# A softmax over heads: summing part of the heads by accumulating transfers

## The chip, the cores and the metric

The kernel runs on one core of a Trainium2 chip. Four of its engines compute: TensorE (PE, with its weight loads as PEld) multiplies matrices into PSUM, VectorE (DVE), ScalarE (ACT) and GpSimd (POOL) work on elements. SyncE (SP) issues transfers, and so can ACT and POOL. Each engine works through its own queue in order and waits on semaphores for the others. The metric is device time in microseconds; the median of three runs counts.

## The reference

The program is four layers, each a cross-attention and a feed-forward network, over 1024 tokens of 128 features and a context of 6404 tokens. The change touches the attention of layer 2 only. What is special in it is that the softmax runs over the 16 heads (axis 1), and not over the keys:

```
qh, kh, vh = split_heads(q @ Wq.T), split_heads(k @ Wk.T), split_heads(v @ Wv.T)   # 16 heads of 8
scores = einsum('bhqd,bhkd->bhqk', qh, kh) / sqrt(8)
attn   = softmax(scores, axis=1)                  # over the heads
heads  = einsum('bhqk,bhkd->bhqd', attn, vh)
x      = x + merge_heads(heads) @ Wo.T
```

So for each key and each query there are 16 exponentials, and all 16 must be summed before any of them can be divided by the sum.

## The kernel before

The function is attn_heads. The work is cut into steps: 1024 queries are two halves of 512 (HALF), the 6404 keys are 51 blocks of 128 (the last has 4), so there are N = 102 steps. A step holds 16 tiles of 128 keys by 512 queries, one for each head. It goes through K = 8 slots, and a slot k handles a pair of heads, 2k and 2k+1. The exponentials of four heads share one tile, so a step has four tiles e0 to e3 of 128 x 2048 float32, each with two buffers.

The loop over slots is a software pipeline written out by hand: under manual_schedule the engines TensorE, ScalarE, VectorE and GpSimd execute in the order in which the program calls them, and nothing is moved by a planner. In one turn of the loop, for slot number `slot` (step i, pair k), these are called:

- least_made: 11 slots ahead, TensorE makes rough scores in bfloat16 in a PSUM tile (pair_ps, one buffer of two banks), and ScalarE casts them to the tile lb (three buffers; L1461). least_so_far: VectorE keeps the smallest over the heads (low, L1469; mneg at the end of a step, L1474). This shifts the exponent for safety.
- exps: TensorE makes the scores of the pair (x_ps, two buffers; L1548) and adds the shift through an identity matmul (L1552). ScalarE takes the exponential into e (L1555).
- first_summed (L1564): TensorE adds one head to a PSUM bank (s_ps) by a matmul with the identity. It takes one head in each slot, eight in a step: heads 0 to 5, 10 and 11 of the 16.
- summed: VectorE adds the other four pairs: pairs 3 and 4 into acc (L1579), then pair 6 and pair 7 onto it (L1582), then folds the two halves of acc (L1585) and adds them to sum (L1586).
- out_of_bank (L1591): in slot 1 of the next step ScalarE copies the bank s_ps into sum.
- inverted (L1598, L1599): ScalarE takes the logarithm of the sum and exp of minus that; improved (L1604, L1605): one Newton step on VectorE. This is 1 / sum.
- shared (L1611): VectorE multiplies a tile e of four heads by it, in every second slot, from slot SHARED = K + 3 of the step on.
- values (L1618): in every second slot from VALUES = K + 6 on, TensorE multiplies such a tile by the values of its heads (vz, spread by ScalarE at L1535) into o_ps. make_values (L1521) makes the values of four steps at a time.

Keys are loaded from DRAM by SyncE two steps ahead (load_keys, L1508). In the second half of the loop the feed-forward network of the first half of the tokens is called between the slots (along); its norm has one small POOL instruction (rstd, L116). POOL does nothing else in the loop but two memsets of a key tile for the blocks of 4 keys (L1506). All 8 PSUM banks are taken: two by pair_ps, four by x_ps, one each by o_ps and s_ps.

Of the kernel before, what the change touches and what calls it, by code (L numbers as in the profile page):

```python
# [10 lines left out]
F32 = mybir.dt.float32  # L11
# [5 lines left out]
ALU = mybir.AluOpType  # L17
# [3 lines left out]
P = 128  # L21
S = 1024
NT = S // P
HALF = 512
# [3 lines left out]
NH = 16  # L28
# [18 lines left out]
class Net:  # L47
# [1317 lines left out]
    def attn_heads(self, ctxT, tiles, before, along):  # L1365
# [13 lines left out]
        nc, tc, a = self.nc, self.tc, self.a  # L1379
# [4 lines left out]
        K = NH // 2  # L1384
        scale = 8.0**-0.5
        with ExitStack() as st:
# [51 lines left out]
            steps = [(c, at, n, half) for half in range(2) for c, (at, n) in enumerate(keys)]  # L1438
            N = len(steps)
            lows, mnegs, es, accs, sums, firsts, invs, kts, outs = ({} for _ in range(9))  # L1440
# [5 lines left out]
            def least_made(slot):  # L1446

                i, k = divmod(slot, K)
                c, at, n, half = steps[i]
                m = self.pair_tile()  # L1450
                for t, (j, r) in enumerate(heads(k)):
                    nc.tensor.matmul(  # L1452
                        m[:n, t], kb[r, at : at + n], qn[r, j, ts(half, HALF)],
                        start=True, stop=True,
                    )
                if k == 0:
                    lows[i] = lp.tile([P, 2, HALF], BF16, tag="low", name="low")
                    t = lows[i]
                else:
                    t = lp.tile([P, 2, HALF], BF16, tag="lb", name="lb", bufs=3)  # L1460
                nc.scalar.copy(t[:n], m[:n])  # L1461
                return t
# [21 lines left out]
            pr = self.pool(st, "a2p", 2)  # L1484
# [3 lines left out]
            ps_s = self.pool(st, "a2ps_s", space=PSUM)  # L1488
# [13 lines left out]
            def load_keys(i):  # L1502
                _, at, n, _ = steps[i]
                kts[i] = pr.tile([P, 4, P], F32R, tag="kS", name="kS", bufs=3)
                if n < P:
                    nc.gpsimd.memset(kts[i].bitcast(F32), 0.0)  # L1506
                for g in range(4):
                    nc.sync.dma_start(  # L1508
                        out=kts[i][32 * g : 32 * g + 32, :, :n].bitcast(F32),
                        in_=kst[P * g : P * g + P, at : at + n].rearrange(  # L1510
                            "(j r) n -> r j n", j=4
                        ),
                    )
# [23 lines left out]
            def pair(i, k):  # L1537
                at = 2 * (k % 2)
                return es[i, k // 2][: steps[i][2], at : at + 2]

            def exps(slot):
                i, k = divmod(slot, K)
                c, at, n, half = steps[i]
                if k % 2 == 0:
                    es[i, k // 2] = e_tile(k // 2)
                s = ps_x.tile([P, 2, HALF], F32, tag="x", name="x_ps")
                for t, (j, r) in enumerate(heads(k)):
                    nc.tensor.matmul(  # L1548
                        s[:, t], kts[i][r, j], qS[r, j, ts(half, HALF)], start=True, stop=False
                    )  # L1550
                for t in range(2):
                    nc.tensor.matmul(  # L1552
                        s[:, t], self.identb, mnegs[i], start=False, stop=True
                    )
                nc.scalar.activation(pair(i, k), s[:n], AF.Exp)  # L1555

            def first_summed(slot):

                i, k = divmod(slot, K)
                if k == 0:  # L1560
                    firsts[i] = ps_s.tile([P, HALF], F32, tag="s", name="s_ps")
                n = steps[i][2]
                h = k if k < 6 else k + 4
                nc.tensor.matmul(  # L1564
                    firsts[i], self.ident[:n], es[i, h // 4][:n, h % 4],
                    start=k == 0, stop=k == K - 1,
                )

            def summed(slot):

                i, k = divmod(slot, K)
                if k == 0:
                    i -= 1
                if i < 0:
                    return
                n = steps[i][2]
                if k == 4:
                    accs[i] = pr.tile([P, 2, HALF], F32, tag="acc", name="acc")
                    nc.vector.tensor_tensor(accs[i][:n], pair(i, 3), pair(i, 4), ALU.add)  # L1579
                elif k in (6, 7):  # L1580
                    acc = accs[i][:n]
                    nc.vector.tensor_tensor(acc, acc, pair(i, k), ALU.add)  # L1582
                elif k == 0:
                    acc = accs[i][:n]
                    nc.vector.tensor_tensor(acc[:, 0], acc[:, 0], acc[:, 1], ALU.add)  # L1585
                    nc.vector.tensor_tensor(sums[i][:n], sums[i][:n], acc[:, 0], ALU.add)  # L1586

            def out_of_bank(i):
                n = steps[i][2]
                sums[i] = pr.tile([P, HALF], F32, tag="sum", name="sum", bufs=1)  # L1590
                nc.scalar.copy(sums[i][:n], firsts.pop(i)[:n])  # L1591

            def inverted(i):

                n = steps[i][2]
                invs[i] = pr.tile([P, HALF], F32, tag="inv", name="inv")
                r, t, s = invs[i][:n], accs[i][:n, 0], sums[i][:n]
                nc.scalar.activation(t, s, AF.Ln)  # L1598
                nc.scalar.activation(r, t, AF.Exp, scale=-1.0)  # L1599
# [13 lines left out]
            def values(i, j):  # L1613
                c, at, n, half = steps[i]
                if c == 0 and j == 0:
                    outs[half] = ps_o.tile([P, HALF], F32, tag="o", name="o_ps")
                for g in range(4):
                    nc.tensor.matmul(  # L1618
                        outs[half][32 * g : 32 * g + 32],
                        vz[i % 2][:n, ds(P * j + 32 * g, 32)], es[i, j][:n, g],  # L1620
                        start=c == 0 and j == 0, stop=c == NK - 1 and j == 3,
                    )
                if c == NK - 1 and j == 3:
                    ob = lp.tile([P, HALF], F32, tag="q32", name="ob")
                    nc.scalar.copy(ob, outs[half])
                    y = self.m_tile()
                    for t in range(4):
                        nc.tensor.matmul(
                            y[:, ts(t, P)], ob[:, ts(t, P)], wo, start=True, stop=True
                        )  # L1630
                    self.add_to_tokens(y, half)

            SHARED = K + 3
            VALUES = K + 6
            SLOTS = N * K
            kept = {}
            other = make_queries(1)
# [3 lines left out]
            for slot in range(SLOTS + 3 * K):  # L1641
                i, k = divmod(slot, K)
                if k == 0 and i + 2 < N:
                    load_keys(i + 2)
                if 1 <= i <= N and k == 1:
                    out_of_bank(i - 1)
                if slot + AHEAD < SLOTS:
                    kept[slot + AHEAD] = least_made(slot + AHEAD)
                if slot < SLOTS:
                    exps(slot)  # L1650
                if 0 < slot <= SLOTS:
                    first_summed(slot - 1)
                at = slot - VALUES
                if 0 <= at < SLOTS and at % 2 == 0:
                    values(at // K, at % K // 2)
                if 0 <= at + 2 < SLOTS and (at + 2) % K == 0:
                    spread_values((at + 2) // K)
                if 0 <= at + 5 < SLOTS and (at + 5) % (4 * K) == 0:
                    make_values((at + 5) // K)
                if slot - 1 + AHEAD in kept:  # L1660
                    least_so_far(slot - 1 + AHEAD, kept.pop(slot - 1 + AHEAD))
                if 0 < slot <= SLOTS + 1:
                    summed(slot - 1)
                if 1 <= i <= N and k == 2:
                    inverted(i - 1)
                if 1 <= i <= N and k == 3:
                    improved(i - 1)
                at = slot - SHARED
                if 0 <= at < SLOTS and at % 2 == 0:
                    shared(at // K, at % K // 2)  # L1670
                if 2 <= i < NK:
                    next(other, None)
                elif i >= NK + 4 and k % 2 == 0:
                    if next(along, None) == "other table":
                        exp_and_ln()
# [425 lines left out]
```

## Time and profile before

| What | Value |
|---|---|
| Time, median of three runs | 6065.93 us (6054.96 to 6070.65) |
| The profiled execution, its own time | 6077.67 us |
| Its span, first to last instruction | 6076.0 us |
| Busy in the span: PE, DVE, ACT, POOL | 91%, 79%, 69%, 16% |
| Mean granted clock of TensorE | 0.957 |
| First and last exponential of the loop (L1555) | 2413.9 and 4573.4 us |
| The loop's sums on TensorE, L1564 | 1632 rows, 850.4 us |
| Additions on VectorE, L1582 (4 of the 204 have 4 rows) | 204, 1216 ns each |
| Copies out of the bank, L1591 | 102, 593 ns each |
| POOL's own transfers (queue q0), whole program | 17.22 MB |

A float32 matmul shows as two rows in the profile, so 1632 rows are 816 sums, eight in each of 102 steps. A row that follows another on the same engine may start before the first has ended by the record, as the engines overlap the end of one instruction with the beginning of the next. For that reason the cost of an instruction in a full queue is read from start to start. In the answers "idle before" gives how long the engine stood before an instruction, and behind the arrow who released it. The granted clock is the share of full speed at which TensorE was allowed to run.

### The profile page before, as it was taken

To read this page: it belongs to the slowest core of one execution; us is meant where nothing else is said; L and a number is where in the kernel's file an instruction comes from. 1 tells how busy PE (TensorE), PEld (TensorE's weight loads), DVE (VectorE), ACT (ScalarE), POOL (GpSimd) and SP (SyncE) were. 2 spreads that over 40 slices of the span, in tenths; PEclk is the share of its full clock that TensorE was granted. 3 is DMA by queue.
4 is the path that set the end of the run, shared out by engine and by line. 5 is a ranking of instruction groups with operands and counts; after the bars stand their busy time and mean duration, and the time that the engine had idled before them with its cause. 6 is when DMAs were issued, how large, how long until landed. Compare 5 with 4: busy or idle time off the path is not lost. (4 is left out here: it accounts for less than half of the span.)

```text
span 6076.0 us, 77642 instructions
## 1 busy us (share of the span) xinstructions
PE 5513.2 (91%) x30144; PEld 2099.9 (35%) x30144; DVE 4771.1 (79%) x5417; ACT 4202.4 (69%) x5284; POOL 964.6 (16%) x687
## 2 busy tenths in 40 slices
PE   6999988899999998999999988899996899999987
PEld 2333335333333345333333322333332333333334
DVE  5555535888888844999999999999997888888834
ACT  3555544677777775888888877788874677777764
POOL 4888883100000010000000000000002000000001
PEclk9999998899999998999999999999996899999978
DMA  0000011100011041000000000000002100011001
GB/s 18 3 2 3 1 40 60 31 14 14 14 18 17 7 150 47 13 13 15 13 15 13 11 13 9 13 15 13 15 8 65 34 14 14 15 18 18 6 16 41
DMA packets 139333, 130.02 MB, mean 21 GB/s; under 512 B 30750, under 2 KB 120278, under 8 KB 137983
## 3 DMA queue, kind: packets, MB, share of 16 engines
q1 hardware_dynamic: 129894, 103.35, 7.8%
q0 software_dynamic: 5296, 17.22, 0.9%
q8 instruction: 239, 3.92, 0.3%
q10 hardware_dynamic: 3760, 4.36, 0.2%
q14 instruction: 144, 1.17, 0.1%
HBM read 102.18 MB, written 35.85 MB: 23 GB/s over the span
## 5 line engine op out<-in xcount | busy, mean ns | idle before, releaser
L994 DVE TENSOR_REDUCE mx<-pair_ps 128x2 f32<-128x1024 f32 x1612 | 1810.5, 1176 | 251.8 <-PE pair_ps L990 229.7
L1223 ACT ACTIVATE px<-x_ps 128x1024 f32<-128x1024 f32 x1088 | 1113.8, 1024 | 312.9 <-PE x_ps L1218 308.4
L1611 DVE TENSOR_TENSOR e<-e,inv 128x2048 f32<-128x2048 f32 (+1 forms) x408 | 932.0, 2285 | 10.8 <-DVE inv L1605 0.9
L1108 PE MATMUL o_ps<-px,v 128*32 128x512 f32 x4352 | 905.8, 621 | 0.0
L1108 PE MATMUL o_ps<-py,v 128*32 128x512 f32 x2176 | 898.3, 618 | 0.0
L990 PE MATMUL pair_ps<-kb,qz 64*128 64x512 bf16 (+1 forms) x3224 | 826.5, 386 | 53.7 <-DVE mx L994 36.9
L1223 ACT ACTIVATE py<-y_ps 128x512 f32<-128x512 f32 x1088 | 647.6, 595 | 327.2 <-PE y_ps L1218 323.6
L1555 ACT ACTIVATE e<-x_ps 128x1024 f32<-128x1024 f32 (+1 forms) x816 | 843.1, 1033 | 25.4 <-PE x_ps L1552 24.8
L1564 PE MATMUL s_ps<-e,ident 128*128 128x512 f32 (+1 forms) x1632 | 850.4, 603 | 0.3 <-ACT sum L1591 0.2
L1461 ACT CAST lb<-pair_ps 128x1024 bf16<-128x1024 f32 (+1 forms) x714 | 721.0, 1010 | 185.4 <-PE pair_ps L1452 136.1
L1218 PE MATMUL x_ps<-qS,kS 33*128 33x512 f32 x2176 | 713.1, 533 | 124.6 <-ACT px L1223 124.5
L400 POOL TENSOR_TENSOR acc<-acc,pt 128x1024 f32<-128x1024 f32 x256 | 601.9, 2351 | 65.3 <-ACT pt L389 51.0
L342 DVE TENSOR_REDUCE mx<-b_ps 128x2 f32<-128x1024 f32 (+1 forms) x306 | 341.1, 1115 | 344.7 <-PE b_ps L338 344.7
L1218 PE MATMUL y_ps<-qS,kS 33*128 33x512 f32 x1088 | 571.3, 525 | 5.7 <-ACT py L1223 5.7
L1469 DVE TENSOR_TENSOR low<-lb,low 128x1024 bf16<-128x1024 bf16 (+1 forms) x714 | 488.8, 685 | 33.1 <-ACT lb L1461 14.0
L1552 PE MATMUL x_ps<-mneg,identb 128*128 128x512 bf16 x1632 | 500.5, 389 | 0.1
L1452 PE MATMUL pair_ps<-qn,kb 32*128 32x512 bf16 (+1 forms) x1632 | 319.8, 387 | 168.2 <-ACT lb L1461 144.1
L1618 PE MATMUL o_ps<-e,vz 128*32 128x512 f32 (+1 forms) x3264 | 446.4, 620 | 9.8 <-DVE e L1611 9.8
L389 ACT ACTIVATE pt<-x_ps,bias 128x1024 f32<-128x1024 f32 x288 | 305.4, 1110 | 213.5 <-PE x_ps L384 198.5
L1218 PEld LDWEIGHTS x_ps<-qS,kS 33*128 33x128 f32 x2176 | 286.1, 192 | 461.9 <-ACT px L1223 215.9
L1548 PE MATMUL x_ps<-qS,kS 32*128 32x512 f32 x1632 | 418.2, 504 | 0.5 <-ACT e L1555 0.5
L990 PEld LDWEIGHTS <-qz 64*128 64x128 bf16 x3224 | 265.5, 94 | 341.5 <-issue 241.0
(387 smaller groups left out, 6115.5 us busy)
## 6 DMA issues: line engine op xcount, KB each, us to landing
kS<-kst SPq DMA_DIRECT2D x400, 64.0 KB
kS<-kd SPq DMA_DIRECT2D x120, 200.1 KB
w<-in_L_ffn_w SPq DMA_DIRECT2D x48, 256.0 KB
kst<-kd POOLq DMA_DIRECT2D x24, 512.0 KB, 13.7
kd<-kh SPq DMA_DIRECT2D x12, 512.0 KB
kd<-k SPq DMA_DIRECT2D x12, 512.0 KB
qS<-qd SPq DMA_DIRECT2D x256, 16.0 KB
kb<-in_L_ffn_w SPq DMA_DIRECT2D x16, 256.0 KB
```

The costliest lines, as they stand in the source:

```text
L400: nc.gpsimd.tensor_tensor(accs[u][:n], first[:n], pt[:n], ALU.add)
L990: nc.tensor.matmul(m[:, g, :n], qzs[u][r, ts(t, P)], kb[r, at : at + n], start=True, stop=True,)
L994: nc.vector.tensor_reduce(mxs[u][:, t, b], m[:, :, :n], AX.X, ALU.max)
L1108: nc.tensor.matmul(o[32 * j : 32 * j + 32], v[:, c, ds(VW * h, 32)], pt, start=i == 0, stop=c + 2 >= NK,)
L1218: nc.tensor.matmul(s[:, k], kS[p % 2][r, ts(c, P)], qS[u % 2][r], start=True, stop=True,)
L1223: nc.scalar.activation(pt[:, : len(some)], s[:, : len(some)], AF.Exp)
L1461: nc.scalar.copy(t[:n], m[:n])
L1469: nc.vector.tensor_tensor(low[:n], t[:n], low[:n], ALU.min)
L1552: nc.tensor.matmul(s[:, t], self.identb, mnegs[i], start=False, stop=True)
L1555: nc.scalar.activation(pair(i, k), s[:n], AF.Exp)
L1564: nc.tensor.matmul(firsts[i], self.ident[:n], es[i, h // 4][:n, h % 4], start=k == 0, stop=k == K - 1,)
L1611: nc.vector.tensor_tensor(e, e, r, ALU.mult)
```

## The change

The sum over the 16 heads of a step is divided in another way.

- VectorE adds pairs 0 and 1 into acc (first_added) in slot 2, and no other pair.
- Pairs 2, 3 and 4 are added to acc by three transfers that GpSimd's queue issues in slots 3, 4 and 5, from SBUF to SBUF with accumulation (more_added). Each is 128 rows of 4 KB, 512 KB. Each waits for the one before it, because all three add to the same tile.
- TensorE adds the last six heads, 10 to 15, in the bank: two in slot 6, one in slot 7, two in slot 0 of the next step and one in its slot 1 (late_summed).
- In slot 2 of the next step VectorE, right after the first_added of that step, folds acc and adds it to the bank, which it reads from PSUM directly. ScalarE's copy of the bank is gone.
- inverted, improved, shared and values come one slot later (SHARED = K + 4, VALUES = K + 7).

The diff, without the lines that are only removed text of the old functions:

```diff
+            late_heads = {6: (10, 11), 7: (12,), 8: (13, 14), 9: (15,)}
+            def late_summed(slot):
                 i, k = divmod(slot, K)
+                if k < 2:
+                    i, k = i - 1, k + K
+                if i < 0 or i >= N or k not in late_heads:
                     return
                 n = steps[i][2]
+                for h in late_heads[k]:
+                    if h == 10:
+                        firsts[i] = ps_s.tile([P, HALF], F32, tag="s", name="s_ps")
+                    nc.tensor.matmul(
+                        firsts[i], self.ident[:n], es[i, h // 4][:n, h % 4],
+                        start=h == 10, stop=h == NH - 1,
+                    )
+            def first_added(i):
                 n = steps[i][2]
+                accs[i] = pr.tile([P, 2, HALF], F32, tag="acc", name="acc")
+                nc.vector.tensor_tensor(accs[i][:n], pair(i, 0), pair(i, 1), ALU.add)
+            def more_added(i, k):
+                acc = accs[i][: steps[i][2]]
+                nc.gpsimd.dma_start(out=acc, in_=pair(i, k), accum_op=ALU.add)
+            def summed(i):
+                n = steps[i][2]
+                acc = accs[i][:n]
                 sums[i] = pr.tile([P, HALF], F32, tag="sum", name="sum", bufs=1)
-                nc.scalar.copy(sums[i][:n], firsts.pop(i)[:n])
+                nc.vector.tensor_tensor(acc[:, 0], acc[:, 0], acc[:, 1], ALU.add)
+                nc.vector.tensor_tensor(sums[i][:n], firsts.pop(i)[:n], acc[:, 0], ALU.add)
...
-            SHARED = K + 3
-            VALUES = K + 6
+            SHARED = K + 4
+            VALUES = K + 7
...
-                if 1 <= i <= N and k == 1:
-                    out_of_bank(i - 1)
...
-                if 0 < slot <= SLOTS:
-                    first_summed(slot - 1)
+                late_summed(slot)
...
-                if 0 < slot <= SLOTS + 1:
-                    summed(slot - 1)
+                if i < N and k == 2:
+                    first_added(i)
+                if i < N and k in (3, 4, 5):
+                    more_added(i, k - 1)
                 if 1 <= i <= N and k == 2:
+                    summed(i - 1)
+                if 1 <= i <= N and k == 3:
                     inverted(i - 1)
-                if 1 <= i <= N and k == 3:
+                if 1 <= i <= N and k == 4:
                     improved(i - 1)
```

More of the change, by code (lines that the diff above doesn't have):

```diff
@@ L1555, in exps @@
                 nc.scalar.activation(pair(i, k), s[:n], AF.Exp)
-            def first_summed(slot):
+            late_heads = {6: (10, 11), 7: (12,), 8: (13, 14), 9: (15,)}
+            def late_summed(slot):
                 i, k = divmod(slot, K)
[L1560 to L1574, printed above, removed]
+                if k < 2:
+                    i, k = i - 1, k + K
+                if i < 0 or i >= N or k not in late_heads:
                     return
                 n = steps[i][2]
[L1577 to L1586, printed above, removed]
@@ L1588, in out_of_bank @@
-            def out_of_bank(i):
-                n = steps[i][2]
+                for h in late_heads[k]:
[6 more added lines that the diff above has]
+            def first_added(i):
+                n = steps[i][2]
+                accs[i] = pr.tile([P, 2, HALF], F32, tag="acc", name="acc")
+                nc.vector.tensor_tensor(accs[i][:n], pair(i, 0), pair(i, 1), ALU.add)
```

## The prediction

> **What bounds the kernel now.** I read the page's slices first, then the loop by stretches, then VectorE, ScalarE and TensorE of two steps in order of time, then the transfers. The loop runs from 2413 to about 4591 us, slices 16 to 30 of 152 us each.
>
> ```profile
> DVE  5555535888888844999999999999997888888834
> ...
> PEclk9999998899999998999999999999996899999978
> ```
>
> By stretch (length, then busy us and instructions of PE, PEld, DVE, ACT, POOL, then clock, DMA share, GB/s):
>
> ```profile
> 2700.00:3300.00 600.00, 559.88 (x2895) 190.41 (x2893) 583.42 (x562) 506.51 (x600) 0.00 (x0) 1.00 0.06 14
> 3420.00:3900.00 480.00, 416.26 (x2034) 144.34 (x2035) 448.23 (x529) 356.67 (x422) 2.02 (x2) 0.95 0.05 12
> ```
>
> ```profile
> 3023.06 1.22 DVE L1579 TENSOR_TENSOR acc<-e,e 128x1024 f32<-128x1024 f32 x1
> ...
> 3027.00 1.22 DVE L1582 TENSOR_TENSOR acc<-acc,e 128x1024 f32<-128x1024 f32 x1
> 3028.13 2.28 DVE L1611 TENSOR_TENSOR e<-e,inv 128x2048 f32<-128x2048 f32 x1
> ...
> 3043.32 1.22 DVE L1579 TENSOR_TENSOR acc<-e,e 128x1024 f32<-128x1024 f32 x1
> ```
>
> One step is 3043.32 - 3023.06 = 20.26 us, and VectorE starts something new as soon as it can in all of it: 97% busy. The other two wait for it, and for each other:
>
> ```profile
> 3034.19 0.63 ACT L1598 ACTIVATE acc<-sum 128x512 f32<-128x512 f32 x1 [1.14 <-DVE sum L1586]
> 3034.85 0.63 ACT L1599 ACTIVATE inv<-acc 128x512 f32<-128x512 f32 x1
> 3035.39 0.99 ACT L1461 CAST lb<-pair_ps 128x1024 bf16<-128x1024 f32 x1
> 3036.28 1.03 ACT L1555 ACTIVATE e<-x_ps 128x1024 f32<-128x1024 f32 x1
> ```
>
> ```profile
> 3036.43 0.39 PE L1452 MATMUL pair_ps<-qn,kb 32*128 32x512 bf16 x2 [1.54 <-ACT lb L1461]
> 3036.44 0.50 PE L1548 MATMUL x_ps<-qS,kS 32*128 32x512 f32 x2
> 3036.87 0.61 PE L1552 MATMUL x_ps<-mneg,identb 128*128 128x512 bf16 x2
> 3037.32 1.02 PE L1564 MATMUL s_ps<-e,ident 128*128 128x512 f32 x2
> 3038.27 1.06 PE L1618 MATMUL o_ps<-e,vz 128*32 128x512 f32 x8
> 3039.26 0.39 PE L1452 MATMUL pair_ps<-qn,kb 32*128 32x512 bf16 x2
> ```
>
> There is one pair_ps tile, so TensorE begins no slot before ScalarE's cast of the slot before has ended. The starts give its prices: scores 0.88 (36.43 to 37.32), a head's sum 0.96, values 0.99. Each of 8 slots has one sum: 8 x 1.84 + 4 x 0.99 = 18.7 us, plus the 1.54 us stall.
>
> **The change part by part.** *VectorE.* Two of three 1.22 us additions go, 1.13 us each from start to start (27.00 to 28.13): 20.26 - 2.26 = 18.0 us. The last addition reads PSUM in place of SBUF; PSUM rows of that shape take 0.68 to 0.69 (L696, L1801), as L1586 now: nothing, and VectorE's slack covers it. *ScalarE.* The copy out of the bank goes, 0.59 us; 506.5 / 600 x 20.26 - 0.6 = 16.5 us are left. *TensorE.* Two of eight sums go: 18.7 - 1.9 = 16.8 us.
>
> If only totals counted, the step would be 18.0 us. But the sums also move: none in slots 2 to 5, two in 6, one in 7, two in 0, one in 1. TensorE's slots 6, 7, 0, 1 cost 2.80, 2.83, 2.80, 2.83; 2 to 5 cost 0.88 or 1.87. ScalarE needs 1.83 a slot (cast 0.91, exponential 0.92), plus logarithm and inverse (0.65 + 0.54) in slot 3. With one pair_ps tile neither can run ahead, so the slow one of each stretch counts. The ring: head 10's sum waits for slot 5's exponential; six sums, three scores, two values bring TensorE to slot 2, 6 x 0.957 + 3 x 0.88 + 2 x 0.993 = 10.4; then 0.43 until the cast starts; ScalarE through slots 2 to 5, 3 x 1.83 + 1.19 + 0.91 + 1.03 = 8.6; 0.05 back. That is 19.5 us. Every fourth step's value matmuls now fall into slot 2 and put about 0.5 us into it: 19.6 on average, 0.66 below now.
>
> *TensorE's clock.* In slot 4 TensorE now waits 2.1 us (ScalarE's two slots and the inverse, 4.9, less 0.88 + 1.87), and what lies around the gap are scores, which fill little of the array. The clock record of this trace changes only on a grid of 3.413 us (all 84 changes). I weighed every matmul row by the share of the array's rows and columns it uses: in the loop, intervals that the half clock followed had 0.40 or less, the others 0.43 or more. That busy time is not what counts, this shows:
>
> ```profile
> 4555.00:4560.00 5.00, 5.00 (x10) 1.46 (x8) 1.67 (x2) 2.07 (x3) 0.00 (x0) 0.50 0.00 0
> ...
> 3439.00:3442.00 3.00, 3.00 (x21) 0.91 (x20) 3.00 (x3) 2.97 (x5) 0.00 (x0) 1.00 0.00 0
> ```
>
> Both are fully busy, with sums over 4 rows; the first, at half clock, has no pair_ps matmuls beside them. Now each step's interval with the 1.54 us stall has about 0.50, just enough. With 2.1 us inside, 1.3 us are left at three quarters or less: 0.3. The grid drifts against the step, so about half the steps get such an interval ((3.4 - 2.1 + 0.4) / 3.4), and the next 3.4 us run at half, 1.7 us of TensorE's ring: +0.85. I take 20.45 us, 0.19 above now; bounds 19.6 (no drop) and 21.3 (one every step).
>
> [...]
>
> *The transfers.* 102 x 3 on POOL's queue, 512 KB each, every one behind the one before since all add into acc. No row shows an adding transfer.
>
> ```profile
> kst<-kd POOLq DMA_DIRECT2D x24, 512.0 KB, 13.7
> ...
> kd<-kS POOLq DMA_DIRECT2D x12, 256.0 KB, 2.5
> ```
>
> Low bound 2.5 us each, by half the bytes; high 13.7, though those 28 came in a burst of 73 us, 2.6 us apiece. Nearest is kd, out of SBUF in 128 rows: that stage moved 227 GB/s at a DMA share of 0.69, so 329 GB/s at full; 256 KB is 0.8 us of the 2.5. An adding transfer reads 1 MB: 1.7 + 3.2 + the 0.5 us issue = 5.4; three 16.2 us. The fold L1589 waits for the last, a whole step after the first addition: 20 us. Hidden, with room up to 6.6 each. *Behind them on POOL:* three rstd (1.0 us) and two memsets of kS; these stand between a third and a first transfer, where the queue waits for nothing but VectorE. SP's key loads stay in place, two steps ahead, at 6% of DMA.
>
> *A slot later.* vz, e and inv are read a slot later, from buffers that come free before their next writer in TensorE's order. At the end one slot more, 2.8 us, and the last step's three transfers beside five short slots: +6 together.
>
> *Sum.* 82 steps of 102 are like the two shown: 82 x 0.19 = +16. Some 20 steps (480 us at 24.0) carry the feed-forward's VectorE chunks, clock 0.95: between -2.3 each (VectorE's relief) and +1.7 (a lost half interval); I take 0. Plus 6: +22. The profiled execution, 6077.7, would be 6100; the median, 11.7 lower, 6088.
>
> **Rivals.** *A, the clock holds.* 82 x -0.66 = -54, 20 x -1.2 = -24, +6: 5994. For it: stalls of 1.89 us twice passed at 1.00 (3697, 3824). Against: those intervals had 0.49 and 0.43, sums on both sides. This one ends on the other side; it decides where an interval with the stall keeps over 0.42. *B, the transfers are exposed.* If three take longer than a step, VectorE stands at L1589; the next step's first addition is already done just before it, so two steps take 3d + 19.5. At d = 7.0 that is 20.3, even with now; at d = 10 (2.5 us per 256 KB read) 24.8, +458: 6524; at 8.5, 22.5 plus a drop, about 6370. For it: no adding row at all, and issues beside VectorE's two-input operations were not seen. Against: d = 5.4. *C, VectorE's total decides.* 18.0 us: -230, 5836. Against it: the ring, which needs a second pair_ps tile to break.
>
> **How the numbers follow.** Something within 0.3% (18 us) can't be told from no change. My forecast, transfers hidden and the clock dropping: 0.40, own range 6040 to 6115; of it 0.07 faster, 0.13 same, 0.20 slower. A 0.16, C 0.03, both faster. B 0.38, slower; 0.13 of it over 6420. 0.03 for nothing at all, same. Faster 0.26, same 0.16, slower 0.58. The range 5985 to 6420 leaves out 0.07 below and 0.13 above.
>
> **What would show it.** The step near 20.5 us; VectorE under 90% busy in 2700 to 3300; TensorE's one stall of about 2 us in slot 4, waiting for ScalarE's cast; the half clock some 30 to 50 times in the loop; acc transfers landing 5 to 6 us after issue and no wait at L1589. Wrong if the clock stays at 1.00 with that stall (A), if L1589 waits for a DMA (B), or if TensorE's stalls vanish (C).

## The result, and the profile after

| | Median | Runs | Against the kernel before, 95% interval |
|---|---|---|---|
| Kernel before | 6074.26 us | 14 (6054.96 to 6085.48) | 1 |
| The change | 6088.14 us | 14 (6071.01 to 6102.57) | 1.0024 (1.0013 to 1.0035) |

The change is 0.24% slower: 14 us, and the interval reaches from 8 to 21. The profiled executions stand the other way round. The change's span is 6069.1 us, 6.9 below that of before. Loop and rest have to be read apart there. From its first exponential (L1555) to the end of its last value matmul the loop takes 2179.0 us before and 2189.1 us after, 10.1 more. In code that the change does not touch, the piece in front of it goes from 2413.9 to 2407.8 us and the piece behind it from 1483.0 to 1472.2; over all profiles of this study these pieces lie between 2407 and 2424 and between 1472 and 1488 us. So the span of a single execution has the wrong sign here, and the medians and the loop agree.

From the page of the change, VectorE and the granted clock in 40 slices of 152 us:

```profile
DVE  5555535888888844788888888888888888888834
...
PEclk8999989899999998999999988999997899999988
```

In slices 17 to 29, counted from 0, VectorE fell from 9 to 8. The same stretches as before (length, then busy us and instructions of PE, PEld, DVE, ACT, POOL, then clock, DMA share, GB/s), of the change:

```profile
2700.00:3300.00 600.00, 528.61 (x2695) 172.51 (x2746) 517.97 (x500) 487.86 (x567) 75.67 (x88) 0.94 0.45 91
3420.00:3900.00 480.00, 398.91 (x1933) 134.04 (x1960) 412.77 (x494) 351.54 (x407) 53.95 (x63) 0.89 0.37 75
```

No engine is full any more. VectorE is at 86%, TensorE at 88%, ScalarE at 81%, and the clock that was 1.00 in this stretch is 0.94. One step on TensorE, in order of time:

```profile
3006.54 0.38 PE L1552 MATMUL x_ps<-mneg,identb 128*128 128x512 bf16 x1 [0.16 <-issue]
3008.74 0.39 PE L1452 MATMUL pair_ps<-qn,kb 32*128 32x512 bf16 x2 [1.82 <-ACT lb L1461]
3008.74 0.50 PE L1548 MATMUL x_ps<-qS,kS 32*128 32x512 f32 x2
3009.18 1.03 PE L1552 MATMUL x_ps<-mneg,identb 128*128 128x512 bf16 x2
3010.14 1.93 PE L1617 MATMUL o_ps<-e,vz 128*32 128x512 f32 x8
3012.00 0.61 PE L1452 MATMUL pair_ps<-qn,kb 32*128 32x512 bf16 x2
...
3016.79 1.07 PE L1617 MATMUL o_ps<-e,vz 128*32 128x512 f32 x8
```

TensorE waits 1.82 us at the end of slot 4 for ScalarE's cast. Just behind the stall the shift takes 1.03 us and the values 1.93, where the same values need 1.07 in the row 6.6 us later: half clock. VectorE in the same step shows where its time went:

```profile
3021.96 0.69 DVE L1469 TENSOR_TENSOR low<-lb,low 128x1024 bf16<-128x1024 bf16 x1 [2.00 <-ACT lb L1461]
3022.88 1.23 DVE L1578 TENSOR_TENSOR acc<-e 128x1024 f32<-128x1024 f32 x1 [0.23 <-ACT e L1555]
3024.03 0.68 DVE L1589 TENSOR_TENSOR acc<-acc 128x512 f32<-128x512 f32 x1
3024.82 0.69 DVE L1590 TENSOR_TENSOR sum<-s_ps,acc 128x512 f32<-128x512 f32 x1
```

It now waits for casts, 2.00 us as slot 2 begins, behind TensorE's bunched sums. It never waits for a transfer: the fold L1589 starts right behind the first addition. GpSimd's issues of that step, and the landing time of all transfers into acc:

```profile
3005.08 0.86 POOL L1582 DMA_DIRECT2D acc<-e  x1 [10.10 <-ACT e L1555]
3009.97 0.86 POOL L1582 DMA_DIRECT2D acc<-e  x1 [4.04 <-ACT e L1555]
3015.50 0.86 POOL L1582 DMA_DIRECT2D acc<-e  x1 [4.67 <-DVE e L1610]
```

```profile
acc<-e POOLq DMA_DIRECT2D x300, 512.0 KB, 4.4
```

The third is issued at 3015.50 and lands some 5 us later, about 3 us ahead of the fold at 3024.03.

The clock can be followed interval by interval. All 192 entries of the change's clock record begin on a grid of 3.413 us. Four intervals of it (columns as above):

```profile
3005.80:3009.21 3.41, 1.44 (x14) 0.62 (x12) 3.27 (x5) 3.38 (x5) 0.14 (x1) 1.00 0.78 154
3009.21:3012.62 3.41, 3.41 (x16) 0.59 (x14) 3.34 (x4) 2.41 (x4) 0.86 (x1) 0.50 0.38 77
3026.28:3029.69 3.41, 2.46 (x16) 0.55 (x15) 3.21 (x4) 3.38 (x5) 0.55 (x1) 1.00 0.76 151
3029.69:3033.10 3.41, 2.82 (x20) 0.99 (x21) 3.34 (x4) 3.41 (x6) 0.86 (x1) 1.00 0.29 56
```

The interval with the stall (first row, 1.44 us busy) is followed by one at 0.50. In the next step the stall is shorter, 1.38 us, and the grid cuts it apart; the third row has 2.46 us busy, and the clock holds in the fourth. A drop begins 16 to 18 us behind an L1474 (the least exponent of a step, on VectorE, one in each step), so its cost shows in the step behind it: 39 of the 42 steady steps from about 2500 us on last 20.8 to 21.1 us from one L1474 to the next where a drop went before, and 19.3 to 19.7 where none did. The record has 70 half-clock stretches in the loop (13 before), 20 of them in the 29.3 steps between 2700 and 3300.

### The profile page after: what moved, and what is told of

Its sections match the earlier page's. It is cut to its first block, busy times and chain, and to the rows that moved or that the text cites. A ratio compares the mean times of both kernels' runs of the same rounds, so it can differ in the third digit from the quotient of the medians.

```text
span 6069.1 us, 76899 instructions
## 1 busy us (share of the span) xinstructions
PE 5389.3 (89%) x29558; PEld 2033.6 (34%) x29736; DVE 4563.6 (75%) x5213; ACT 4154.7 (68%) x5182; POOL 1228.1 (20%) x993
## 3 DMA queue, kind: packets, MB, share of 16 engines
q0 software_dynamic: 48688, 174.62, 14.2%
## 5 line engine op out<-in xcount | busy, mean ns | idle before, releaser
L1555 ACT ACTIVATE e<-x_ps 128x1024 f32<-128x1024 f32 (+1 forms) x816 | 844.4, 1035 | 15.6 <-PE x_ps L1552 10.4
L1582 POOL DMA_DIRECT2D acc<-e x306 | 263.5, 861 | 1940.6 <-ACT e L1555 1366.8
L1570 PE MATMUL s_ps<-e,ident 128*128 128x512 f32 (+1 forms) x1224 | 605.5, 604 | 0.9 <-issue 0.2
L1452 PE MATMUL pair_ps<-qn,kb 32*128 32x512 bf16 (+1 forms) x1632 | 335.3, 405 | 244.7 <-ACT lb L1461 216.2
L1552 PE MATMUL x_ps<-mneg,identb 128*128 128x512 bf16 x1454 | 484.5, 407 | 29.0 <-issue 29.0
L1617 PE MATMUL o_ps<-e,vz 128*32 128x512 f32 (+1 forms) x3264 | 495.0, 682 | 3.9 <-DVE e L1610 3.9
L1548 PE MATMUL x_ps<-qS,kS 32*128 32x512 f32 x1632 | 430.5, 523 | 4.8 <-ACT e L1555 4.8
```

The costliest lines, as they stand in the source:

```text
L1570: nc.tensor.matmul(firsts[i], self.ident[:n], es[i, h // 4][:n, h % 4], start=h == 10, stop=h == NH - 1,)
L1617: nc.tensor.matmul(outs[half][32 * g : 32 * g + 32], vz[i % 2][:n, ds(P * j + 32 * g, 32)], es[i, j][:n, g], start=c == 0 and j == 0, stop ...
```

## The experiments

Theory: TensorE's and ScalarE's ring, stretched by the bunched sums, and the clock drops that its stall brings, give back what VectorE gained; the transfers cost nothing. Rivals: the transfers slow something after all; the clock goes by idle time or by busy time and not by how much of the array is filled; VectorE's relief was smaller than worked out. All kernels below are the change with one edit. In the table "step" is the mean of 42 steps without feed-forward, from L1474 to L1474 (from about 2500 us on), "drops" the half-clock stretches that begin between 2700 and 3300 us. The ratios go by the runs of the kernel before on the same chip, with medians of 6068.7 to 6075.7 us.

| Kernel | Median us | Ratio to before, 95% | Step us | Drops |
|---|---|---|---|---|
| before | 6074 | 1 | 20.27 | 0 |
| the change | 6088.1 | 1.0024 (1.0013 to 1.0035) | 20.48 | 20 |
| fill, 128 rows | 5991.5 | 0.986 (0.9842 to 0.9878) | 19.43 | 0 |
| fill64 | 6007.2 | 0.989 (0.987 to 0.9909) | 19.46 | 0 |
| fill32 | 6055.2 | 0.9969 (0.9958 to 0.998) | 20.04 | 11 |
| fill4 | 6087.0 | 1.0021 (1.0008 to 1.0034) | 20.48 | 19 |
| no_transfers | 6085.8 | 1.0013 (1.0 to 1.0027) | 20.44 | 19 |
| longer | 6132.3 | 1.0096 (1.0078 to 1.0115) | 20.85 | 18 |
| on_vector | 6189.3 | 1.0192 (1.0168 to 1.0216) | 21.27 | 18 |
| twice | 6747.9 | 1.1111 (1.1081 to 1.1142) | 27.40 | 22 |
| even | 5866.6 | 0.9653 (0.9638 to 0.9668) | 18.05 | 0 |

### A filler in the stall

```diff
-                    if h == 10:
-                        firsts[i] = ps_s.tile([P, HALF], F32, tag="s", name="s_ps")
...
+            def filled(i):
+                n = min(steps[i][2], 128)
+                firsts[i] = ps_s.tile([P, HALF], F32, tag="s", name="s_ps")
+                nc.tensor.matmul(
+                    firsts[i], self.ident[:n], es[i, 0][:n, 0], start=True, stop=True
+                )
...
                 late_summed(slot)
+                if i < N and k == 4:
+                    filled(i)
```

> The change, with one more matmul of TensorE in each step: at the end of slot 4, where TensorE stands for ScalarE's cast, it multiplies head 0's exponentials by the identity (128 rows, one sum's price, 0.96 us) into the bank s_ps, and the first real sum in slot 6 overwrites that. Theory (the clock gives the gain back: the stalled interval fills too little of the array, half clock follows): the filler lifts that interval from about 0.36 to over 0.6 of the array, the clock holds, the step falls from 20.48 to the ring's 19.6 us, 82 x 0.88 = 72 us: about 6016 us, 0.990 of the kernel before; fewer than 25 half-clock stretches in the loop instead of 70. Rival (the ring of casts and sums is longer than 19.6 for another reason, transfers that slow the engines for instance): no gain, 6088 us, or up to 80 us slower if the filler comes on top.

The stretch 2700 to 3300 of fill, and the filler (L1576) with the stall that is left behind it:

```profile
2700.00:3300.00 600.00, 552.60 (x2901) 186.71 (x2954) 543.23 (x525) 509.96 (x595) 79.31 (x92) 1.00 0.48 95
```

```profile
3001.18 1.02 PE L1576 MATMUL s_ps<-e,ident 128*128 128x512 f32 x2
3002.72 0.39 PE L1452 MATMUL pair_ps<-qn,kb 32*128 32x512 bf16 x2 [0.53 <-ACT lb L1461]
3002.73 0.50 PE L1548 MATMUL x_ps<-qS,kS 32*128 32x512 f32 x2
3003.39 0.38 PE L1552 MATMUL x_ps<-mneg,identb 128*128 128x512 bf16 x1 [0.16 <-issue]
3003.70 1.06 PE L1622 MATMUL o_ps<-e,vz 128*32 128x512 f32 x8
```

A matmul whose result nobody reads makes the kernel 97 us faster (6088.1 to 5991.5). The clock is 1.00, and the values behind the stall need 1.06 us and not 1.93. The step falls by 1.05 us, 0.17 more than expected, since the ring at full clock is 19.43 us long and not 19.6; the median is 25 us below the 6016 expected.

### The same duration, another share of the array

The edit is 4 (fill4), 32 (fill32) or 64 (fill64) in the place of 128.

> The same filler at the same place and of the same duration, but it contracts over 4 rows instead of 128: TensorE is as busy as in the other, and fills 1/32 of the array. Theory (the share of the array counts): the half clock stays, at least 60 stretches in the loop, step near 20.5 us, about 6088 us, 1.002 of the kernel before. Rival (idle gaps count, the clock drops because TensorE stands): the gap falls from 1.8 to under 1 us, the clock holds, 6016 us as with the full filler.

Two pairs of grid intervals of fill4 (columns as above):

```profile
3018.75:3022.16 3.41, 2.47 (x16) 0.97 (x14) 3.27 (x5) 3.38 (x5) 0.06 (x1) 1.00 0.78 154
3022.16:3025.57 3.41, 3.41 (x15) 0.54 (x14) 3.34 (x4) 2.46 (x5) 0.86 (x1) 0.50 0.43 86
3039.23:3042.64 3.41, 3.38 (x18) 0.85 (x17) 3.21 (x4) 3.38 (x5) 0.43 (x1) 1.00 0.78 156
3042.64:3046.05 3.41, 2.94 (x20) 1.06 (x21) 3.34 (x4) 3.41 (x6) 0.86 (x1) 1.00 0.20 38
```

The first row has 2.47 us of busy TensorE, no less than the row at 3026.28 of the change (2.46), after which the clock held. Here it drops. By these rows busy time is not what counts, and by the waits the idle gap is not either. TensorE's wait for the cast in 2700 to 3300 (line, releaser, us in total, times, longest), first of fill4, then of fill:

```profile
PE pair_ps L1452 <- ACT lb L1461: 28.3, 50, 0.8
PE pair_ps L1452 <- ACT lb L1461: 37.7, 55, 1.0
```

With gaps of 0.8 us at most fill4 has 19 drops, nearly as many as the change with gaps of 1.8; fill, with gaps of up to 1.0, has none.

> The filler in slot 4 over 32 rows, a quarter of the array: 0.957 / 4 = 0.24 us of full array in an interval of 3.41 us, so the stalled interval rises from about 0.36 (0.35 to 0.42) to 0.43. Theory (a share of the array of about 0.42 over a fixed interval of 3.413 us decides): this stands right at the edge, and most of the drops go: 5991 to 6040 us, fewer than 35 half-clock stretches in the loop (71 in the change, 16 with the full filler). Rival (busy time and rows count in some other way, or much more than 0.43 is needed): 60 or more stretches and 6085 us, as over 4 rows.

> The filler over 64 rows, half the array: 0.48 us of full array, the stalled interval rises from about 0.36 (0.35 to 0.42) to 0.50. With 32 rows, at 0.43, about half the drops were left. Theory (the share of the array counts, edge near 0.42): all of an interval's margin is there, no drop in the stretch from 2700 to 3300 us, step 19.4 to 19.5, 5991 us as with the full filler. Rival (the number of rows that a matmul uses, not their sum over the interval, must be full for the clock to hold): some drops stay, 6010 us or more.

With 32 rows about half the drops go (45 half-clock stretches are left in the loop, where fewer than 35 were expected) and the time lies between, 15 us above the range expected. I weighed each matmul by rows times columns used, over the 128 x 128 of the largest rows, per grid interval: in fill32 intervals at 0.43 and 0.44 still dropped, and some at 0.38 and 0.41 held. In the change all 22 that dropped between 2600 and 3300 had 0.28 to 0.42 and all others 0.43 or more. By this estimate the edge is at about 0.42 with some 0.04 to either side, which may be my weighing. With 64 rows no drop is left in that stretch and the step is that of fill. The median is 16 us above it, so the expected 5991 was missed; in the profiled executions the two loops differ by 3.7 us of 13.5, and the rest lies outside the loop.

### Without the transfers

```diff
-                if i < N and k in (3, 4, 5):
-                    more_added(i, k - 1)
```

> The change without its three adding transfers: pairs 2, 3 and 4 are missing from the sum, so the output is another; all else stays. Theory (transfers hidden, ring and clock set the step): no wait and no duration on the path changes, about 6088 us, 1.002 of the kernel before, between 6075 and 6100; step 20.48 us. Rival (the transfers slow the engines' access to SBUF, or hold buffers): the step falls below 20.2 us, the kernel under 6065 us.

The stretch of no_transfers:

```profile
2700.00:3300.00 600.00, 528.84 (x2717) 172.31 (x2766) 519.13 (x501) 490.09 (x570) 0.00 (x0) 0.95 0.06 13
```

Against 528.61, 172.51, 517.97 and 487.86 with them. A DMA share of 0.45 and 91 GB/s beside the engines made nothing longer that could be measured: the means of VectorE's and ScalarE's groups in this stretch are the same within 4 ns.

### The additions back on VectorE

```diff
-                nc.gpsimd.dma_start(out=acc, in_=pair(i, k), accum_op=ALU.add)
+                nc.vector.tensor_tensor(acc, acc, pair(i, k), ALU.add)
```

> The change, with the three transfers undone: VectorE itself adds pairs 2, 3 and 4 in slots 3, 4 and 5. TensorE's bunched sums, the PSUM read and the later slot stay. Theory (the transfers are what takes the bound from VectorE): VectorE needs 18.04 + 3 x 1.13 = 21.4 us a step and is full again, the ring of 19.5 is hidden behind it: 82 x (21.4 - 20.26) = 94, and 20 mixed steps by about 1.1: 6190 us, 1.019 of the kernel before. Rival (VectorE's additions are not worth 1.13 us each in the step, or drops of the clock still add to it): 6110 or less, or 6230 and more.

```profile
2700.00:3300.00 600.00, 516.70 (x2609) 169.33 (x2658) 588.25 (x565) 471.19 (x543) 0.00 (x0) 0.94 0.06 13
```

6189.3 where 6190 was expected, in part by luck, since the step is 21.27 us and not 21.4: VectorE is at 98%, and each addition is worth 1.07 us (a third of 21.27 - 18.05, the step of even, below), nearly the 1.13 worked out, as long as VectorE is the bound. The clock drops nearly as often as in the change (18 times to 20) and costs nothing there: the steps there are 21.26 us long with a drop or without. So the transfers take 3.2 us a step from VectorE (21.27 to 18.05), and the change could use 0.8 of it.

### Twice the transfers

```diff
-                nc.gpsimd.dma_start(out=acc, in_=pair(i, k), accum_op=ALU.add)
+                for _ in range(2):
+                    nc.gpsimd.dma_start(out=acc, in_=pair(i, k), accum_op=ALU.add)
```

> The change with each of the three transfers issued twice, six chained adding transfers a step (pairs 2, 3 and 4 count twice in the sum, the output is another). Theory of the exposed rival in the prediction: with d from issue to issue 4.9 to 5.6 us, on average 5.25, VectorE stands at the fold L1589, and two steps take 6d + 19.5 = 51 us, 25.5 a step: 5.0 us more than 20.48 in about 100 steps, near 6590 us, 1.085 of the kernel before. Rival (six transfers follow one another freely, one step 6 x 5.25 = 31.5 us): 7190 us. Rival (transfers overlap and land together): no change, 6088 us.

VectorE's wait in 2700 to 3300 (line, releaser, us in total, times, longest), then one step's issues on GpSimd, of twice:

```profile
DVE acc L1590 <- DMA acc<-e: 165.2, 22, 10.9
```

```profile
2912.41 1.75 POOL L1583 DMA_DIRECT2D acc<-e  x2 [3.79 <-DMA acc<-e]
2919.62 0.86 POOL L1583 DMA_DIRECT2D acc<-e  x1 [5.46 <-DMA acc<-e]
2924.59 0.86 POOL L1583 DMA_DIRECT2D acc<-e  x1 [4.11 <-DMA acc<-e]
2929.85 0.86 POOL L1583 DMA_DIRECT2D acc<-e  x1 [4.40 <-DMA acc<-e]
2935.17 0.86 POOL L1583 DMA_DIRECT2D acc<-e  x1 [4.46 <-ACT lb L1461]
2939.86 1.75 POOL L1583 DMA_DIRECT2D acc<-e  x2 [3.83 <-DMA acc<-e]
```

The wait at the fold is what the exposed rival describes, but the formula fell, between its two branches: 27.4 us a step, not 25.5 or 31.5. The first transfer of a step goes into the other buffer of acc and is issued together with the last one of the step before (x2). So a step is the distance of six issues less one that is shared, 2912.41 to 2939.86. The 42 steps have 26.4 to 30.3 us each, and VectorE waited 22 times in 21.9 steps, once in every step: two steps do not share one wait.

### The ring a little longer

```diff
                 nc.scalar.activation(t, s, AF.Ln)
+                nc.scalar.activation(r[:, :P], t[:, :P], AF.Exp, scale=-1.0)
                 nc.scalar.activation(r, t, AF.Exp, scale=-1.0)
```

> The change, with ScalarE taking the second half of the inverse (L1598) once more for 128 of its 512 columns: about 0.25 us on ScalarE's slot 3, which lies in the ring of casts and sums. Theory lock (drops come on a fixed grid of 3.413 us, and the step settles at six intervals, 20.48 us, by dropping as often as that needs): the step stays within 0.05 of 20.48 us, with fewer half-clock stretches than 70 or as many; the kernel within 8 us of 6088 in the steady steps. Rival (each step simply adds its lost time to the ring): the step grows by the 0.25 us, to 20.7 us: 82 x 0.25 = 20, 6108 us.

Both expectations fell. The added instruction takes 0.31 us by its row, and the step grew by 0.37. From L1474 to L1474 eight steps repeat: 23.08, 21.22, 21.06, 19.68, 21.65, 19.67, 19.68, 21.20, in sum 167.24 us, which is 49 x 3.413. In the change twelve steps repeat, 245.84 us or 72 x 3.413, a mean of exactly six intervals. In this stretch steps and grid do fall into a common period, but not into the six-interval step that I expected to hold. Why this period and not another stays open.

### The same work, spread

```diff
-            late_heads = {6: (10, 11), 7: (12,), 8: (13, 14), 9: (15,)}
+            late_heads = {4: (6, 7), 6: (10, 11), 8: (14, 15)}
...
-                if i < N and k in (3, 4, 5):
+                if i < N and k in (3, 5, 7):
                     more_added(i, k - 1)
```

(The sum starts at head 6.)

> The change with its parts spread over the step: TensorE sums heads 6 and 7 in slot 4, 10 and 11 in slot 6, 14 and 15 in slot 0 of the next step, each time in a slot without value matmuls; the transfers add pairs 2, 4 and 6 in slots 3, 5 and 7. As many sums, additions and transfers as in the change. Theory (what the change lost is the bunching of its sums, by the ring and then by the clock; the transfers are harmless): no stretch of slots is long on TensorE and on ScalarE in turn, the array is filled in every interval, and VectorE's 18.0 us bound the step: 18.0 to 18.5, so 82 x 2.0 to 2.5 plus some 20 us in the mixed steps, 5865 to 5905 us, 0.966 to 0.972 of the kernel before, nearly no half clock in the loop. Rival (transfers cost, or the PSUM read on VectorE does): VectorE waits at the fold for the last transfer, which is issued only three slots earlier, or the step stays above 19.5: 6010 us or more.

The stretch of even, one step of VectorE, and the only wait of its fold for a transfer between 2700 and 3300 us:

```profile
2700.00:3300.00 600.00, 572.86 (x3071) 187.19 (x3123) 582.53 (x566) 551.94 (x642) 86.00 (x100) 1.00 0.51 102
```

```profile
3001.03 1.22 DVE L1578 TENSOR_TENSOR acc<-e 128x1024 f32<-128x1024 f32 x1
3002.16 0.68 DVE L1589 TENSOR_TENSOR acc<-acc 128x512 f32<-128x512 f32 x1
3002.95 0.69 DVE L1590 TENSOR_TENSOR sum<-s_ps,acc 128x512 f32<-128x512 f32 x1
3003.56 2.28 DVE L1610 TENSOR_TENSOR e<-e,inv 128x2048 f32<-128x2048 f32 x1
```

```profile
DVE acc L1589 <- DMA acc<-e: 0.2, 1, 0.2
```

5866.6 us, 3.5% faster than before, with the same sums, additions and transfers as the change. VectorE is at 97% again, now in a step of 18.05 us, TensorE at 95% and ScalarE at 92%, and the clock is 1.00. TensorE's double sums stand in slots 4, 6 and 0, which have no value matmuls; where the change stalled for 1.82 us there is a sum, and what stall is left at L1452 is 0.5 us at most.

## Why the prediction was right, point by point

- **VectorE's relief, 2.26 us a step: right (2.2 measured).** Where VectorE bounds, the step is 18.05 us (even) against the 18.0 worked out, so the PSUM read (L1590, 0.69 us) costs nothing more than the SBUF read before (L1586, 0.69 us).
- **The ring, 19.5 or 19.6 at full clock: right, 0.15 too long.** fill and fill64 show 19.43 and 19.46. The stall itself is 1.38 to 1.82 us and not 2.1.
- **The clock: the share of the array counted, as taken (no drop with the filler over 128 rows, 19 with the same over 4); both sizes were off.** I took half of the steps and 1.7 us each, +0.85. Measured: 20 drops in 29.3 steps, 0.68 a step, and 20.48 - 19.45 = 1.03 a step, so 1.5 us for each drop. The 30 to 50 half-clock stretches forecast were 70, of which 13 were there before. The step of 20.45 us came out at 20.48 by luck, since this error and that of the ring nearly cancel. The stall is not much longer than the 1.54 us of before, after which no interval dropped in this stretch: what is missing beside it are the full-array sums, which left slots 2 to 5.
- **Transfers hidden: right, with the price too high.** They land after 4.4 us (5.4 taken), and the issue takes 0.86 us (0.5 taken); issue to issue is 4.9 to 5.5 in the rows above. No run shows the 1 MB that an adding transfer was taken to read: POOL's queue q0 moved 157.4 MB more than before (174.62 less 17.22) for 306 transfers, 512 KB for each of the 300 full ones. Without the transfers the step is 20.44 us, against 20.48.
- **The sum, +22: the sign right, the size too large.** The loop measured +10.1 and the medians +14 (8 to 21). The forecast of 6088 us was met to 0.2 us by luck: it starts from the first three runs of the kernel before, 6065.93, and the 14 runs have 6074.26, so that the base was 8 us too low and the step from it 8 us too high. By pieces, from L1474 to L1474: the steady steps +13.0 (8.7 in the 42 from about 2500 us on, 4.3 in the 33 behind the feed-forward), where 82 steps were to give +16. The mixed steps, taken as nothing, gave -5.3 (21 of them, 500.9 to 495.6). The three steps before the steady ones gave +12.3 and were in no term of the sum: between 2462 and 2502 us VectorE waits 14.3 us for the queries of the second half (L1432 behind ScalarE's L1431), and 4.4 before. All nine other kernels have these steps slow too (the last of the three 35 us or more, 29.3 before), even among them; the cause was not tried alone. For the later slot and the tail the sum had +6; the last step gave +3.6, and from the last L1474 to the end of the last value matmul the loop is 13.5 us shorter than before:

```profile
4540.58:4592.90 52.32, 48.68 (x158) 10.72 (x156) 37.25 (x26) 14.21 (x20) 0.20 (x1) 0.63 0.00 1
4558.09:4596.90 38.81, 34.06 (x155) 8.65 (x156) 31.23 (x21) 12.02 (x17) 3.46 (x5) 0.86 0.13 23
```

The first row is before, the second the change (columns as above). The last step has 4 keys, and its sums fill 4 rows of the array. Before, the clock was at half for 38.3 us of this piece, in the change for 10.7. That fits what the fillers showed (19 drops with 4 rows, none with 128), but it is one execution of each and was not tried alone.

- **Rival A, the clock holds, 5994 us.** Its price was about right: 72 us below the 6066 that it starts from, and with the filler the kernel ran 5991.5, 84 below the 6075.7 of before on that chip. Its condition, over 0.42 of the array in the interval with the stall, is where my weighing of the three smaller fillers puts the edge. The change fails it.
- **Rival B, transfers exposed.** It did not happen. Its formula, two steps in 3d + 19.5, was wrong; twice shows one wait in every step.
- **Rival C, VectorE's total decides.** It did not happen in the change. The claim that only a second pair_ps tile could break the ring was wrong: spreading the same sums over the slots was enough, and even is that rival, within 31 us of its 5836.

## What to carry to other kernels

When work is taken from the full engine, look at which slots the remaining work of the others falls into: here, with one buffer between two engines, neither averaged over the step, and six sums in four slots made a step of 20.48 us, the same six spread out one of 18.05. A TensorE stall cost twice here, once itself (1.4 to 1.8 us) and once by the half clock behind it (about 1.5 us for each drop), where it left the 3.413 us interval filled to 0.42 or less by my weighing, so try to put full-array work that has to be done anyway into the stall. Judge a change of 0.2% by the stage that it touches and by many runs; one execution's span had the wrong sign.

## What the runs showed of the hardware that was not expected

- In these runs the drops go by the share of the array, to the point that dead work pays: a 128-row filler of 0.96 us in each step won 97 us and left none of the 20 drops between 2700 and 3300 us; the same filler over 4 rows left 19 and won nothing (6087.0 us to 6088.1), 64 rows left none and gave the step of 128 (19.46 us to 19.43), 32 rows left 11.
- In the steady steps from about 2500 us on, drops and steps fall into a common period: 12 steps in 72 intervals of 3.413 us in the change, 8 steps in 49 with 0.31 us more on ScalarE.
- Three accumulating transfers of 512 KB a step, 91 GB/s in all, slowed no instruction of the other engines that could be measured: the step is 20.44 us without them and 20.48 with them.
